# Order of the last node tiles' steps at the end of layer 2 of a two-layer graph attention kernel

## Chip, cores and metric

The kernel runs on one core of one Trainium2 chip. The metric is the device time of one execution in microseconds (us). The median of three runs of the kernel before is 2619.84 us, from 2609.17 to 2623.1.

## The reference, cut to what matters

A graph of 6250 nodes and 100000 edges, sorted by destination, passes through two graph attention layers and a small network of two dense layers; the input is added at the end.

```python
def gat_conv(x, src, dst, W, a_src, a_dst, bias, heads):
    h = (x @ W).reshape(n, heads, -1)
    alpha_s = (h * a_src[None]).sum(-1)
    alpha_d = (h * a_dst[None]).sum(-1)
    e = leaky_relu(alpha_s[src] + alpha_d[dst], 0.2)
    e = exp(e - segment_max(e, dst)[dst])
    alpha = e / (segment_sum(e, dst)[dst] + 1e-16)
    return segment_sum(h[src] * alpha[:, :, None], dst).reshape(n, -1) + bias
...
h = relu(layernorm(x))
h = relu(gat_conv(h, src, dst, W1, a_src1, a_dst1, b1, 4))   # 768 -> 256, 4 heads
h = relu(gat_conv(h, src, dst, W2, a_src2, a_dst2, b2, 1))   # 256 -> 256, 1 head
h = relu(h @ Wm1 + bm1)                                      # 256 -> 256
x = x + h @ Wm2 + bm2                                        # 256 -> 768
```

Each node has an edge to itself beside the others. All numbers are float32.

## The kernel before

The nodes lie in 49 tiles of 128 (NT = 49; the last, tile 48, holds 106 nodes). The edges lie in 784 tiles of 128, four to a group, so 196 groups (NG = 196) and four groups to a node tile. A first stage computes layer 1's features and stores them as a table of rows in device memory. Then `layer_edges` runs twice, for layer 1 and for layer 2, once over all groups each time.

In the loop of `layer_edges` over g, a group is worked on as follows.

- `gather(g + 8)` lets GpSimd (POOL) fetch the source rows of the group eight ahead, one indirect DMA for each tile of 128 edges (line 553). So the last gather is issued when g is 187, as far as the code goes.
- `pair(g, 0)` and `pair(g, 1)` take two edge tiles each: two exponentials on ScalarE (ACT; lines 620 and 622), a product, a maximum and two one-hot matrices weighted by the attention on VectorE (DVE; lines 625, 628 and 632), and two matmuls into `o_ps[g]` on TensorE (PE; line 648). In the profile, each float32 matmul stands as two records.
- `gather_up(g)` adds the group's result to a running sum (line 673) and copies a quarter of a node tile from it (line 681). When a tile's fourth quarter is there, its steps are put at the end of the list `late`. For the last group it puts the steps of the last tile, 48, there instead.
- `advance(g)` goes through `late` and lets each tile there take one piece of its steps. It is called twice in a group, and in groups 192 and 193 it goes through the list twice at each call.

What a tile does after its sum is the generator `Node2.steps`. It is cut by `yield`; the pieces are called A to F here, in program order:

- A: `all_` and its denominator `rden`, on DVE (line 896, or 906 for the last tile, and line 908).
- B: `o` on ACT (line 911), two transposes into `tp` on PE (line 761), and for the last tile the two bias rows of its outputs (line 873).
- C: `rT` on ACT (line 767), then the first dense layer on PE (line 921; "mm1" below).
- D: `mT` on ACT (line 926), then on PE, for the first half of the columns, the bias row (line 873) and two matmuls into `y_ps` (line 937).
- E: the first half's addition of the input on DVE (line 940), then bias row and matmuls of the second half on PE. A tile other than the last uses the same `y_ps` for both halves, so these wait for the addition.
- F: the second half's addition on DVE, then the tile's output DMA on SyncE's queue (SP; line 946). The last tile sends each half by itself, the first on SP at E and the second on ACT's queue at F (line 943).

After B, C, D and E stands `yield from rest(3)`: three calls of `advance` pass, the one that ran the piece among them, before the next piece is run, or one once the list `at_end` is not empty.

Nothing is reordered by a scheduler: the block runs under `tc.manual_schedule()`, and each engine gets its instructions in the order in which the Python code emits them. That order around the end of layer 2, with the calls written out, is:

```
g=193: pair(193,0) | 45 F, 46 C | pair(193,1) | 46 D | sums 191, 192
g=194: pair(194,0) | sum 193 | 46 E, 47 A | pair(194,1) | 46 F, 47 B
g=195: pair(195,0) | pair(195,1) | sum 194 | 47 C | 47 D
after: 47 E, 48 A | 47 F, 48 B | 48 C | 48 D | 48 E | 48 F
```

PSUM has two buffers for `tp` and `y_ps` of all tiles but the last (tag "n"), and three for `o_ps` and the last tile's two `y_ps` (tag "o"). The working tiles (`all_`, `o`, `rT`, `mT`, `y`) have two buffers each.

Of the kernel before, what the change touches and what calls it, by code (L numbers as in the profile page):

```python
# [30 lines left out]
NG = NQ  # L31
# [22 lines left out]
def kernel(  # L54
# [184 lines left out]
    def first_sources(layer):  # L239

        n = len(THERE[layer])
        sources[layer] = []
        for j in range(0, n, 8):
            m = min(n - j, 8)
            of = rowsp.tile([P, 16 * P], BF16, name="drow").bitcast(I32)
            nc.sync.dma_start(of[:, :m * P], bcast(src_rows, m * P, (FIRST + j) * P))
            sources[layer].append(of)
# [269 lines left out]
    def fetch_rows(r):  # L517

        if r < NET // 16:
            drow[r] = rowsp.tile([P, 16 * P], BF16, name="drow")  # L520
            nc.sync.dma_start(drow[r], bcast(dmod_d, 16 * P, r * 16 * P))
# [7 lines left out]
    def layer_edges(layer, H, node, pre, matched, pre_pool):  # L529
# [4 lines left out]
        with tc.tile_pool(name=f"eg{layer}", bufs=4) as eg, \  # L534
# [9 lines left out]
            def gather(g):  # L544
                if not 0 <= g < NG:
                    return
                for t in tiles(g):
                    k = TPG * g + t
                    if k // 2 not in G:
                        G[k // 2] = first_G[layer].get(k // 2) or rows_in(layer)  # L550
                    if k < FIRST + len(THERE[layer]):
                        continue
                    nc.gpsimd.indirect_dma_start(  # L553
                        out=G[k // 2][:, k % 2], out_offset=None, in_=table[layer],
                        in_offset=bass.IndirectOffsetOnAxis(ap=src_i[:, k:k + 1], axis=0))
# [5 lines left out]
            def make_mask(u):  # L561

                if not 0 <= u < NU:
                    return
                if layer == 2:
                    return fetch_mask(u + 1)
                a, b = (t * P for t in both(u))
                mask[u] = maskp.tile([P, 8 * P], BF16, name="mask")
                if u == 0:
                    nc.vector.memset(mask[u][:, :a], 0.0)  # L570
                at = u % 2 * 8 * P
                nc.vector.tensor_scalar(mask[u][:, a:b], drow[u // 2][:, at + a:at + b], pidx, None,  # L572
                                        ALU.is_equal)
                nc.sync.dma_start(mask_d[u * P:(u + 1) * P], mask[u])

            def make_hot(g):

                if layer == 2 or not 0 <= g < NG:
                    return
                T = tiles(g)  # L580
                k, n = TPG * g + T[0], len(T)
                hot[g] = eg.tile([P, TPG, P], F32, name="hot")
                nc.vector.tensor_tensor(  # L583
                    hot[g][:, T[0]:T[0] + n], iota_ps.unsqueeze(1).to_broadcast([P, n, P]),
                    dcol[:, k:k + n].unsqueeze(2).to_broadcast([P, n, P]), ALU.is_equal)
# [7 lines left out]
            def meet(t):  # L593

                if t >= NT:
                    return
                e_ps[t] = ps.tile([P, 16, 6 * H], F32, name="e_ps", tag="e")
                for u, at, a, b in ranges(t):
                    m = mask.pop(u)
                    for k in range(a, b):  # L600
                        nc.tensor.matmul(e_ps[t][:, at + k, :3 * H], m[:, k * P:(k + 1) * P],  # L601
                                         pre.win[:, 2 * u + k // TPG + 1], start=True, stop=True)

            def join(t):
                if t >= NT:
                    return
                (_, _, a, _), (_, at, _, b) = ranges(t)
                T = slice(a, at + b)
                nc.vector.tensor_reduce(
                    e_ps[t][:, T, 3 * H:4 * H],  # L610
                    e_ps[t][:, T, :3 * H].rearrange("p t (h k) -> p t h k", k=3), AX.X, ALU.add)
# [39 lines left out]
            def stay_warm(n):  # L651

                if layer == 1:
                    for _ in range(n):
                        nc.tensor.matmul(idle_ps[0], idle[:, :P], idle, start=True, stop=True)

            done, run, late, idle_ps = {}, {}, [], []

            def gather_up(g):

                if not 0 <= g < NG:
                    return
                last = g == NG - 1
                if last:

                    late.append(node.steps(NT - 1, None, run[0], o_ps.pop(g)))
                    return
                acc = sums.tile([P, RW[layer]], F32, name="acc")
                if g == 0:
                    nc.vector.tensor_copy(acc, o_ps.pop(g))  # L670
                else:
                    k = (g + 1) % 4
                    nc.vector.scalar_tensor_tensor(acc, run[0], keep[:, k:k + 1],  # L673
                                                   o_ps.pop(g), ALU.mult, ALU.add)
                run[0] = node.whole(NT - 1, acc) if g == NG - 2 else acc
                t, q = divmod(g - 2, 4)
                if 0 <= t < NT - 1:
                    if q == 0:
                        done[t] = sums.tile([P, RW[layer]], F32, name="sum", bufs=3)
                    r = slice(32 * q, 32 * q + 32)  # L680
                    nc.scalar.activation(done[t][r], acc[r], AF.Copy)  # L681
                    if q == 3:
                        late.append(node.steps(t, done.pop(t)))

            def advance(g):

                for _ in range(2 if NG - 4 <= g < NG - 2 else 1):
                    for step in list(late):
                        if next(step, 0) == 0:
                            late.remove(step)  # L690
# [14 lines left out]
            join(0)  # L705
            for g in range(NG):
                t, j = divmod(g, 4)
                if g == NG - 2:
                    at_end.append(g)
                gather(g + AHEAD)  # L710
                pair(g, 0)
                if g == NG - 1:
                    pair(g, 1)
                if g >= NG - 2:
                    gather_up(g - 1)
                advance(g)
                if g <= NG - 4:
                    make_hot(g + 1)
                if g in (NG - 4, NG - 3):
                    make_hot(g + 2)  # L720
                if j == 0:
                    if layer == 1:
                        fetch_rows(t + 4)
                    node.prefetch(t)
                    meet(t + 1)
                elif j == (2 if t < NT - 1 else 1):
                    node.ahead(t)
                elif j % 2:
                    make_mask((g + 7) // 2)
                if g == NG - 3:  # L730
                    idle_ps.append(ps.tile([P, 4 * P], F32, name="idle_ps", tag="e"))
                if g >= NG - 3:
                    stay_warm(3)
                if g < NG - 1:
                    pair(g, 1)
                advance(g)
                if j == 3:
                    join(t + 1)
                if g < NG - 2:
                    gather_up(g - 2)  # L740
                if g == NG - 3:
                    gather_up(g - 1)
                if NG - 3 <= g < NG - 1:
                    stay_warm(3)
                hot.pop(g, None)
                if layer == 1 and g == NG - 6:
                    first_sources(2)
            gather_up(NG - 1)
            advance(NG)
            stay_warm(4)  # L750
            if layer == 1:
# [19 lines left out]
    with tc.tile_pool(name="w2p", bufs=1) as wp, tc.tile_pool(name="wk2", bufs=2) as wk:  # L771
# [48 lines left out]
        with tc.tile_pool(name="pre1", bufs=1) as pre:  # L820
            first_hits(pre, 1, 0)
            pre1 = prepare(pre, 1, 4)
            layer_edges(1, 4, Node1(), pre1,
                        lambda: scores_in(ps, w2, *w2_in, KH, 1), pre)


    with tc.tile_pool(name="wmp", bufs=1) as wp, tc.tile_pool(name="x3", bufs=4) as xp, \
# [122 lines left out]
        for stage in range(2):  # L950
            first_hits(pre, 2, stage)
        layer_edges(2, 1, Node2(), pre2, matched, pre)

    edges_stack.close()
# [298 lines left out]
```

## Time and profile before

| what | us or value |
|---|---|
| median of three runs | 2619.84 |
| the profiled execution's own time | 2137.04 |
| its span, first to last instruction | 2135.3 |
| mean granted TensorE clock | 0.825 of full speed |
| last row gather issued on POOL | about 2111.6 |
| last matmul pair of group 195 starts | 2116.7 |
| last addition of the output starts (line 940) | 2128.68 |
| last output DMA issued (line 943) | 2129.27 |

Times in the profile count from the span's start. A line of the timeline has the start, the length, the engine, the source line, the operation, the tile it writes and those it reads, shapes and count, and in brackets how long the engine was idle before it and who released it. A line of the table by stretches has the stretch, its length, each engine's busy time and instructions, the granted clock, the share of the DMA engines and GB/s. The profiled execution is shorter than the timed runs by 483 us; the profile does not say why.

### The profile page before, as it was taken

How to read it: one execution, taken by the hardware profiler on the slowest of the kernel's cores; microseconds unless marked ns; L12 is line 12 of the kernel's file. 1: busy time of each engine (PE TensorE's matmuls, PEld its weight loads, DVE VectorE, ACT ScalarE, POOL GpSimd, SP SyncE). 2: the span in 40 equal slices, each digit the busy share in tenths (PEclk: the TensorE clock that was granted, in tenths of full speed). 3: DMA queues.
4: the chain of work that ended last, by engine and by line, in shares of the span. 5: the costliest groups of instructions: out<-in, count | busy, mean ns of one | idle time of the engine just before them, and what ended most of it. 6: DMA issues, size and time to landing. Idle time of an engine off the chain costs nothing.

```text
span 2135.3 us, 26701 instructions
## 1 busy us (share of the span) xinstructions
PE 1589.5 (74%) x6763; PEld 1075.4 (50%) x6765; DVE 1416.1 (66%) x4359; ACT 593.1 (28%) x2601; POOL 1600.6 (75%) x1759
## 2 busy tenths in 40 slices
PE   8996777766767677666768677777767777777777
PEld 6874444444444444444445445545545545545544
DVE  7887777667677777677777655555555555555554
ACT  4651222222222222222222222222222222222222
POOL 6877777777777777777777777777777777777774
PEclk9998888677777767887779888888888888888888
DMA  9976666555555565565556455565555555565553
GB/s 356 363 232 206 169 172 176 165 169 163 167 170 163 170 170 162 169 168 158 166 143 211 130 180 166 169 181 166 169 181 166 169 181 166 169 181 167 168 171 114
DMA packets 157544, 383.26 MB, mean 179 GB/s; under 512 B 35543, under 2 KB 49966, under 8 KB 157382
## 3 DMA queue, kind: packets, MB, share of 16 engines
q0 software_dynamic: 75072, 209.10, 36.6%
q1 hardware_dynamic: 80940, 170.88, 23.1%
q10 hardware_dynamic: 1370, 1.48, 0.2%
q8 instruction: 58, 0.95, 0.2%
q14 instruction: 104, 0.85, 0.1%
HBM read 323.13 MB, written 58.19 MB: 179 GB/s over the span
## 4 chain that ended last, share of the span: by engine, by line
DMA 27%; PE 26%; DVE 26%; issue 9%; ACT 7%; POOL 5%; ACTq 0%; SPq 0%; POOLq 0%; DVEq 0%
DMA G<-table,src_i 26%; PE o_ps L648 11%; DVE hw L637 8%; PE y_ps L937 7%; POOL G L553 4%; PE h_ps L350 4%; DVE acc L673 3%; DVE e_ps L625 3%; ACT sum L681 3%; DVE e_ps L635 2%; ACT e L620 2%; DVE hw L632 2%; DVE mask L572 1%; ACT e L622 1%; PE y_ps L873 1%
## 5 line engine op out<-in xcount | busy, mean ns | idle before, releaser
L553 POOL DMA_INDIRECT G<-table,src_i x1545 | 1470.1, 952 | 472.3 <-issue 260.5
L648 PE MATMUL o_ps<-hw,hot 128*128 128x260 f32 x1564 | 596.7, 520 | 282.9 <-DVE hw L637 221.4
L648 PE MATMUL o_ps<-G,hw 128*128 128x258 f32 x1564 | 469.1, 432 | 229.8 <-DVE hw L632 229.1
L648 PEld LDWEIGHTS o_ps<-hw,hot 128*128 128x128 f32 x1564 | 352.9, 248 | 492.9 <-DVE hw L637 359.2
L625 DVE TENSOR_TENSOR e_ps<-e,e_ps 128x8 f32<-128x8 f32 (+1 forms) x782 | 128.4, 164 | 598.9 <-ACT e L622 597.5
L648 PEld LDWEIGHTS o_ps<-G,hw 128*128 128x128 f32 x1564 | 309.9, 212 | 348.3 <-DVE hw L632 290.5
L681 ACT ACTIVATE sum<-acc 32x260 f32<-32x260 f32 (+1 forms) x384 | 159.9, 416 | 776.9 <-DVE acc L673 775.3
L620 ACT ACTIVATE e<-G 128x8 f32<-128x8 f32 (+1 forms) x782 | 159.9, 204 | 617.8 <-DMA G<-table,src_i 576.4
L632 DVE TENSOR_SCALAR hw<-iota_ps,dcol,w 128x128 f32<-128x128 f32 x782 | 285.0, 406 | 14.4
L637 DVE TENSOR_TENSOR hw<-G,e_ps 128x520 f32<-128x520 f32 x391 | 271.9, 695 | 15.2 <-DVE e_ps L635 2.0
L937 PE MATMUL y_ps<-wm,mT 128*128 128x384 f32 x392 | 206.5, 664 | 0.7 <-ACT mT L926 0.7
L673 DVE SCALAR_TENSOR_TENSOR acc<-acc,keep,o_ps 128x260 f32<-128x260 f32 (+1 forms) x388 | 184.5, 476 | 0.1
L622 ACT ACTIVATE e<-G 128x8 f32<-128x8 f32 (+1 forms) x782 | 148.9, 190 | 0.2
L350 PE MATMUL h_ps<-w,r 128*128 128x256 f32 x588 | 133.0, 380 | 4.4 <-ACT r L341 4.4
L583 DVE TENSOR_TENSOR hot<-iota_ps,dcol 128x512 f32<-128x512 f32 (+1 forms) x196 | 133.5, 682 | 0.0
L937 PEld LDWEIGHTS y_ps<-wm,mT 128*128 128x128 f32 x392 | 88.3, 249 | 66.9 <-issue 40.9
L350 PEld LDWEIGHTS h_ps<-w,r 128*128 128x128 f32 x588 | 108.0, 190 | 21.8 <-ACT r L341 5.7
L635 DVE TENSOR_TENSOR e_ps<-e_ps,e 128x8 f32<-128x8 f32 x391 | 68.1, 174 | 13.4
L365 POOL TENSOR_TENSOR ha<-kept,a1b 128x512 f32<-128x512 f32 x45 | 53.2, 1183 | 23.9 <-ACT kept L356 23.8
L628 DVE TENSOR_TENSOR w<-e_ps,e 128x2 f32<-128x2 f32 x391 | 62.2, 159 | 13.3
L601 PEld LDWEIGHTS <-mask 128*128 128x128 bf16 x1564 | 57.7, 101 | 11.4 <-issue 1.7
L767 ACT ACTIVATE rT<-tp,bT 128x128 f32<-128x128 f32 x196 | 59.4, 352 | 6.6 <-PE tp L761 6.4
(405 smaller groups left out, 1137.7 us busy)
## 6 DMA issues: line engine op xcount, KB each, us to landing
xt<-in_x SPq DMA_DIRECT2D x96, 384.0 KB, 4.8
drow<-dmod_d SPq DMA_DIRECT2D x49, 512.0 KB, 6.4
mask_d<-mask SPq DMA_DIRECT2D x98, 256.0 KB, 2.2
mask<-mask_d SPq DMA_DIRECT2D x98, 256.0 KB, 5.9
G<-table,src_i POOLq DMA_INDIRECT x1545, 2.9
xTt<-in_xT SPq DMA_DIRECT2D x49, 384.0 KB, 5.9
out<-y SPq DMA_DIRECT2D x48, 384.0 KB
table<-kept SPq DMA_DIRECT2D x49, 132.0 KB, 3.7
```

The costliest lines, as they stand in the source:

```text
L350: nc.tensor.matmul(h_ps, r[:, k], w1[:, k], start=(k == 0), stop=(k == KI - 1))
L553: nc.gpsimd.indirect_dma_start(out=G[k // 2][:, k % 2], out_offset=None, in_=table[layer], in_offset=bass.IndirectOffsetOnAxis(ap=src_i[:, ...
L583: nc.vector.tensor_tensor(hot[g][:, T[0]:T[0] + n], iota_ps.unsqueeze(1).to_broadcast([P, n, P]), dcol[:, k:k + n].unsqueeze(2).to_broadca ...
L620: nc.scalar.activation(e1, sc, AF.Exp)
L622: nc.scalar.activation(e2, sc, AF.Exp, scale=SLOPE)
L625: nc.vector.tensor_mul(v, e2, rho)
L632: nc.vector.tensor_scalar(hw[:, t], iota_ps, dcol[:, k:k + 1], w[:, t], ALU.is_equal, ALU.mult)
L637: nc.vector.tensor_mul(hw, Gp[:, :, :RW[1]].rearrange("p t (h c) -> p t h c", h=H), w.unsqueeze(3).to_broadcast([P, 2, H, C + 1]))
L648: nc.tensor.matmul(o_ps[g], l, r[:, :RW[layer]], start=(k == tiles(g)[0]), stop=(k == TPG - 1))
L673: nc.vector.scalar_tensor_tensor(acc, run[0], keep[:, k:k + 1], o_ps.pop(g), ALU.mult, ALU.add)
L681: nc.scalar.activation(done[t][r], acc[r], AF.Copy)
L937: nc.tensor.matmul(y_ps, mT[:, j], wm2[:, j, s * half:(s + 1) * half], start=False, stop=(j == KH - 1))
```

## The change

Only the order of the steps at the end of layer 2 is changed; layer 1 keeps its own. `at_end` is filled one group earlier, at g = 193, which ends the waiting of `rest` there. Group 194 gets a second pass of `advance` after its first, and group 195 loses its second one. After the loop the last tile's first three pieces are run before `advance` comes to the tile before it.

```diff
             for g in range(NG):
                 t, j = divmod(g, 4)
-                if g == NG - 2:
+                if g == (NG - 2 if layer == 1 else NG - 3):
                     at_end.append(g)
...
                 advance(g)
+                if layer == 2 and g == NG - 2:
+                    advance(g)
...
                     pair(g, 1)
-                advance(g)
+                if layer == 1 or g < NG - 1:
+                    advance(g)
...
             gather_up(NG - 1)
+            if layer == 2:
+
+                for _ in range(3):
+                    next(late[-1])
             advance(NG)
```

Followed through the generators by hand, this gives the order:

```
g=193: pair(193,0) | 45 F, 46 C | 46 D | pair(193,1) | 46 E | 46 F | sums 191, 192
g=194: pair(194,0) | sum 193 | 47 A | 47 B | pair(194,1) | 47 C
g=195: pair(195,0) | pair(195,1) | sum 194 | 47 D
after: 48 A, 48 B, 48 C | 47 E, 48 D | 47 F, 48 E | 48 F
```

## The prediction

> **What bounds the kernel now.** I read the page first (part 1 and the costliest groups), then a table of stretches for the end, then the timeline of the last 30 us engine by engine, then the clock in steps of 0.4 us.
>
> ```profile
> PE 1589.5 (74%) x6763; PEld 1075.4 (50%) x6765; DVE 1416.1 (66%) x4359; ACT 593.1 (28%) x2601; POOL 1600.6 (75%) x1759
> ...
> L553 POOL DMA_INDIRECT G<-table,src_i x1545 | 1470.1, 952 | 472.3 <-issue 260.5
> ```
>
> No engine is full. The row gathers set the pace: 0.95 us each and 0.30 us of issue after each, 1.25 us, so 5.0 us for the four gathers of a group and 20 us for a node tile. That pace ends with the last gather:
>
> ```profile
> 2090.00:2111.60 21.60, 16.51 (x56) 10.20 (x55) 11.54 (x41) 6.10 (x26) 16.43 (x18) 0.84 0.62 178
> 2111.60:2129.30 17.70, 15.09 (x61) 8.93 (x60) 8.53 (x25) 4.71 (x17) 0.03 (x1) 1.00 0.19 63
> 2129.30:2135.30 6.00, 0.00 (x0) 0.00 (x0) 0.00 (x0) 0.00 (x0) 0.00 (x0) 0.63 0.16 45
> ```
>
> The columns are length, busy PE, PEld, DVE, ACT, POOL, clock, DMA share, GB/s. After 2111.6 POOL is silent and PE is busy 15.09 of 17.70 us: the tail is a chain through PE with few gaps. The last 6.0 us are the output's landing and the end of the program. Only this tail, of at most 24 us (1.1% of the span), is in reach of the change. Its vector lines, of before, say what stands where:
>
> ```profile
> 2108.34 0.99 DVE L673 SCALAR_TENSOR_TENSOR acc<-acc,keep,o_ps 128x258 f32<-128x258 f32 x2
> 2110.46 0.17 DVE L625 TENSOR_TENSOR e_ps<-e,e_ps 128x2 f32<-128x2 f32 x1 [1.12 <-ACT e L622]
> ...
> 2114.34 0.56 DVE L940 TENSOR_TENSOR y<-y_ps,xt 128x384 f32<-128x384 f32 x1 [0.17 <-PE y_ps L937]
> ...
> 2120.77 0.56 DVE L940 TENSOR_TENSOR y<-y_ps,xt 128x384 f32<-128x384 f32 x1 [2.90 <-PE y_ps L937]
> 2121.25 0.41 DVE L906 TENSOR_TENSOR all__20266<-all__20245,o_ps 128x258 f32<-128x258 f32 x1
> ```
>
> The first two lines are the sums of groups 191 and 192 and the start of group 194; the third is step F of tile 46; the last two are E of tile 47 and, only behind it, A of the last tile, 48. And PE's end:
>
> ```profile
> 2115.66 2.17 PE L648 MATMUL o_ps<-G,hw 128*128 128x258 f32 x8 [0.27 <-DVE hw L632]
> 2117.67 1.05 PE L921 MATMUL tp<-rT,wm 128*128 128x128 f32 x8
> 2118.65 0.33 PE L873 MATMUL y_ps<-bm2r,ones_r 3*128 3x384 bf16 x1
> 2119.18 1.56 PE L937 MATMUL y_ps<-wm,mT 128*128 128x384 f32 x4 [0.19 <-ACT mT L926]
> 2121.38 0.32 PE L873 MATMUL y_ps<-bm2r,ones_r 3*128 3x384 bf16 x1 [0.65 <-DVE y L940]
> 2121.63 1.56 PE L937 MATMUL y_ps<-wm,mT 128*128 128x384 f32 x4
> ```
>
> Group 195 leaves PE at 2117.83 (the chain of waits goes on to mm1 there), and the last addition starts at 2128.68: 10.85 us for tiles 47 and 48, one after the other.
>
> **What the Trainium skill says.** "PSUM — Partial Sum Buffer", Engine vs sequencer instructions: the queues of ScalarE and VectorE are strictly first in, first out, and matmuls start in program order. The trace agrees: every step above stands in each engine's stream where the code emits it, so a waiting instruction holds all behind it. "TensorE: Matmul & The Clock Gate", What's actually happening: the clock is full or half, by activity in a free-running window of about 3.4 us. The trace agrees: 1.0 or 0.5, changes at about 2096.75 and 2103.6, two windows apart. Such windows were busy 1.14 of 3.41 us (33%) just before the half clock of 1854.4, and 1.88 of 3.41 (55%) at 2089.93 without one. That is where I put the threshold.
>
> **The change, part by part.** Layer 1 and everything before group 193 keep their order; no instruction is added or removed, POOL's stream is the same. Letters A to F are the steps of a tile in program order.
>
> 1. Tile 46, group 193: D goes ahead of pair (193,1), and E and F into this group's second advance, ahead of the sums of 191 and 192. Before, PE starts mm1 of tile 46 at 2107.51, and D's mT at 2108.60 lets its output matmuls start 0.42 later, at 2109.02, 1.56 long, to 2110.55. The exponentials of pair (193,1), at 2104.73 before, now queue behind mT on ACT: 2109.25; from there to the pair's first matmul it took 1.19 (2110.13 to 2111.32 for the next pair), so 2110.5, just when PE is free. Pair (193,1) issues for 0.87, to 2111.40. So far this costs about 0.2. E's addition 2110.73 to 2111.29 lies under it. Then E's bias row and matmuls: 0.3 + 1.5, to 2113.2. Now the new wait: F's addition stands at the head of VectorE's queue until 2113.2, and behind it are both sums and all of pair (194,0). From 2113.22: addition 0.56, two sums 0.99, the second sum's copy on ACT 0.46, exponential to matmul 1.19: pair (194,0) starts on PE at 2116.45. Before: 2111.32. **That is +5.13**, with PE empty from 2113.2 to 2116.45.
>
> 2. Group 194: tile 47's B ahead of pair (194,1), C ahead of group 195. Sum of 193 at 2116.63 (0.65 after the pair's hw); from that sum to B's o it took 1.68 before (2111.50 to 2113.18): 2118.31; the next exponential 0.41 later, at 2118.72; + 1.19: pair (194,1) on PE at 2119.91 (before 2114.14). The transposes, 0.38, fit before it. After it PE issues 0.87, C's mm1 0.91 and pairs (195,0) and (195,1), 0.87 each: 2123.43. Their hw are ready (2121.14 and 2122.22 by the same 1.19). Before: 2117.83. So at the end of group 195 the change stands at **+5.60**, though E and F of tile 46 (about 1.8 us of PE) and C of 47 (0.91) are already done.
>
> 3. The end. Tile 47's D has nothing to pass: nothing stands between its old and new place. Its bias row and matmuls, 0.26 + 1.56 = 1.82, go first, with mT long there. Under them A of tile 48 (0.41 + 0.17), its o (0.51) and three hops, about 1.25, are hidden; without that cover they would show in full. Then transposes to rT 0.42, rT to mm1 0.67, mm1 0.91, E's matmuls of tile 47 with the bias row 1.81 (they cover tile 48's mT, and E's addition is long done), tile 48's own 2.86, and 0.02: 8.51 against 10.85. **That is −2.34.**
>
> 4. DMAs. Tile 46's output leaves SP about 1 us earlier; nothing else is in SP's queue there. Tile 47's output moves from 2123.8 to about 2130.8, still ahead of tile 48's on SP, 2 to 3 us before the last one on ACT's queue. Before, its 0.38 MB were moved in about 1.5 us (2124.5 to 2126.0), so it should be over; I take 0, at most +1, and not below nothing, as no transfer gets shorter. Everything else after the last addition stays 6.1 us.
>
> 5. The clock, which no row of before prices here. PE is empty for 3.25 us and again from 2117.5 to 2118.9. Wherever the 3.41 us windows fall, one of them has at most 1.2 us of work, 36%: under the threshold, so the clock should halve between 2114.4 and 2118.8. From 2119.9 PE is full, and by before's records it comes back after one full window: half clock until 2123.3 to 2125.6, half of which, 1.7 to 2.9 us, is lost. I take 2.3; bounds 0 (no halving; a gain is excluded, since nothing runs above 1.0) and 11.4 (rival two).
>
> Sum: 5.60 − 2.34 + 0 + 2.3 = +5.56. The profiled execution took 2137.04 us (span 2135.3 and 1.7 around it), so 2142.6. The runs' median, 2619.84, is 483 us above the profiled execution; nothing in the trace says where these are. I carry the difference over as it is: 2619.84 + 5.56 = 2625.4. Scaled by 2619.84/2137.04 it would be +6.8.
>
> **Rivals.** *The stall is hidden, and the end's gain stays.* If in the timed runs the gathers are what is slow (483 us over 1545 gathers would be 0.31 each), pairs arrive 3.1 us apart, a group takes 6.2, and the 5 us of delay in group 194 lie largely under waits for rows; group 195 ends with its last row, as before. Then −2.3 stays: 2617.5. For it: ACT still waits for rows at 2114.30. Against: in the profile that wait is 0.42.
>
> *The half clock stays to the end*, and the kernel is measurably slower. From 2116.45 on PE has 13.4 us of work (four pairs 3.7, two mm1 1.8, transposes 0.6, output matmuls 6.2, bias rows 1.1). If no window is full, because VectorE and ACT leave gaps, all of it takes twice as long; some 2 us of gaps absorb part: +11.4, with the 3.3 of the stall +14.7: 2634.5. It decides if the gaps for rT and mT fall in every window; before, of the nine halvings after 1936 eight lasted two windows and one a single one, so I give it little.
>
> *Nothing arrives.* Gain and stall cancel, the clock holds, within 1 us: 2620.
>
> **How the numbers follow.** A difference of 0.5%, 13 us, is about what a measurement of this kernel can tell from no change. The forecast (+3 to +7) 0.62, hidden stall 0.23, nothing 0.09, half clock to the end 0.06. Only the last is a change of over 0.5%. The three runs of before spread over 14 us, so a median can stray by 6 or 7: I leave 0.03 for a stray on the good side, and 0.92 for within 0.5%, 0.05 for slower. The range goes from the hidden stall with such a stray (2611) to the half clock (2635).
>
> **What would show it.** In the profile of the changed kernel: F's addition of tile 46 right before the pair of sums, with about 1.9 us of waiting for its matmuls; PE idle some 3.2 us before pair (194,0); clock 0.5 somewhere after 2114; the last tile's A directly after the last sum, before tile 47's E; 8.5 us from the last pair's end to the last addition, or more under the half clock. I am wrong if pair (194,0) starts before 2114, if the clock holds 1.0 after a 3 us gap, or if the last transfer lands later than 6 us after the last addition.

## The result, and the profile after

The changed kernel takes 2621.14 us (median of 20 runs, 2612.03 to 2632.93), the kernel before 2616.84 (20 runs): the medians are 4.3 us apart. The ratio, taken over all runs, is 1.0020 with a 95% interval of 1.0005 to 1.0034. That is 5.2 us, between 1.3 and 8.9; 5.56 were forecast.

One thing must be known before the two profiles are laid side by side. The profiled execution of the changed kernel has a span of 2621.7 us, that of before 2135.3. This is not the change: the same programs take about 2137 us on some chips and 2610 to 2640 on others (the shorter and the longer kind below). The 20 runs of each kernel in the result are all of the longer kind, and each ratio of the experiments is of runs on one chip. Spans from different chips are not compared. What is compared is the tail, from the start of tile 46's first dense layer on PE ("mm1") to the start of the last addition. It took 21.17 us before and 27.01 after: 5.84 more. In the profile before, it begins with these lines (... stands for the lines between), mm1 of tile 46 and, 3.81 us later, the first matmuls of group 194, called pair (194,0) below:

```profile
2107.51 1.05 PE L921 MATMUL tp<-rT,wm 128*128 128x128 f32 x8
...
2111.32 1.14 PE L648 MATMUL o_ps<-G,hw 128*128 128x258 f32 x4
```

PE in the tail of the changed kernel, from the timeline:

```profile
2588.33 1.05 PE L928 MATMUL tp<-rT,wm 128*128 128x128 f32 x8
2589.31 0.33 PE L880 MATMUL y_ps<-bm2r,ones_r 3*128 3x384 bf16 x1
2589.84 1.56 PE L944 MATMUL y_ps<-wm,mT 128*128 128x384 f32 x4 [0.19 <-ACT mT L933]
2591.23 1.03 PE L648 MATMUL o_ps<-G,hw 128*128 128x258 f32 x4
2592.20 0.33 PE L880 MATMUL y_ps<-bm2r,ones_r 3*128 3x384 bf16 x1
2592.46 1.56 PE L944 MATMUL y_ps<-wm,mT 128*128 128x384 f32 x4
2597.18 1.14 PE L648 MATMUL o_ps<-G,hw 128*128 128x258 f32 x4 [3.17 <-DVE hw L632]
2599.60 0.69 PE L768 MATMUL tp<-ident,o 128*128 128x128 f32 x2 [1.28 <-ACT o L918]
2600.63 2.09 PE L648 MATMUL o_ps<-G,hw 128*128 128x258 f32 x4 [0.34 <-DVE hw L632]
```

The line numbers have moved by 7 (L921 is L928, L937 is L944, L940 is L947). The first line is mm1 of tile 46; the two halves of its output follow in the same group, with pair (193,1) between them. Then PE is empty for 3.17 us before pair (194,0), which starts 8.85 us after mm1. So of the 5.04 us by which the pair is later, about 3.2 are this gap, and 1.8 are the matmuls of tile 46's second half (0.33 and 1.56, overlapping), which stood behind the pair before and are now done ahead of it. The last line is pair (194,1), at the half clock: 2.09 us where a pair takes 1.03 to 1.14 at the full clock. VectorE says why PE was empty:

```profile
2591.43 0.56 DVE L947 TENSOR_TENSOR y<-y_ps,xt 128x384 f32<-128x384 f32 x1
2594.05 0.56 DVE L947 TENSOR_TENSOR y<-y_ps,xt 128x384 f32<-128x384 f32 x1 [2.06 <-PE y_ps L944]
2594.53 0.99 DVE L673 SCALAR_TENSOR_TENSOR acc<-acc,keep,o_ps 128x258 f32<-128x258 f32 x2
2596.32 0.17 DVE L625 TENSOR_TENSOR e_ps<-e,e_ps 128x2 f32<-128x2 f32 x1 [0.80 <-ACT e L622]
```

These are E's addition, then F's, which waits 2.06 us for E's matmuls, and behind F the two sums and the first VectorE step of pair (194,0). In the profile before, the two sums stood at 2108.34, right behind pair (193,1).

The stretches of this tail (length, busy PE, PEld, DVE, ACT, POOL, clock, DMA share, GB/s): up to F, the empty stretch, up to the end of group 195, and the end:

```profile
2588.33:2594.05 5.72, 5.50 (x23) 3.08 (x21) 1.61 (x5) 0.81 (x4) 0.00 (x0) 1.00 0.17 69
2594.05:2597.18 3.13, 0.00 (x0) 0.00 (x0) 2.22 (x7) 1.13 (x4) 0.00 (x0) 1.00 0.32 126
2597.18:2607.07 9.89, 8.26 (x27) 6.27 (x27) 5.26 (x18) 2.73 (x12) 0.00 (x0) 0.65 0.01 2
2607.07:2615.34 8.27, 7.95 (x31) 4.41 (x30) 2.26 (x5) 1.76 (x5) 0.00 (x0) 1.00 0.13 50
```

The third stretch has a mean clock of 0.65. In the last one PE is busy 7.95 of 8.27 us: the end has become a chain of PE work, as forecast.

### The profile page after: what moved, and what is told of

Read it like the earlier page. It is cut to its first block, busy times and chain, and to the rows that moved or that the text cites. A ratio compares the mean times of both kernels' runs of the same rounds, so it can differ in the third digit from the quotient of the medians.

```text
span 2621.7 us, 26701 instructions
## 1 busy us (share of the span) xinstructions
PE 1650.0 (63%) x6763; PEld 1116.7 (43%) x6765; DVE 1414.5 (54%) x4359; ACT 560.2 (21%) x2601; POOL 1604.0 (61%) x1759
## 4 chain that ended last, share of the span: by engine, by line
DVE 29%; issue 21%; PE 20%; another core or an unknown queue 19%; ACT 6%; POOL 2%; DMA 2%; ACTq 0%; POOLq 0%; SPq 0%; DVEq 0%
PE o_ps L648 9%; DVE hw L637 8%; DVE hw L632 4%; PE y_ps L944 4%; PE h_ps L350 4%; DVE acc L673 3%; DVE e_ps L625 3%; ACT sum L681 2%; POOL G L553 2%; DVE e_ps L635 2%; ACT e L620 2%; DVE mask L572 2%; DMA G<-table,src_i 2%; DVE hot L583 1%
## 5 line engine op out<-in xcount | busy, mean ns | idle before, releaser
L648 PE MATMUL o_ps<-G,hw 128*128 128x258 f32 x1564 | 497.7, 455 | 177.1 <-issue 90.4
L648 PEld LDWEIGHTS o_ps<-G,hw 128*128 128x128 f32 x1564 | 337.6, 228 | 301.4 <-issue 124.4
L944 PE MATMUL y_ps<-wm,mT 128*128 128x384 f32 x392 | 197.8, 622 | 119.3 <-issue 84.5
L944 PEld LDWEIGHTS y_ps<-wm,mT 128*128 128x128 f32 x392 | 81.7, 228 | 192.6 <-issue 138.8
L947 DVE TENSOR_TENSOR y<-y_ps,xt 128x384 f32<-128x384 f32 (+1 forms) x98 | 54.1, 552 | 127.6 <-remote 73.8
L928 PE MATMUL tp<-rT,wm 128*128 128x128 f32 x392 | 68.1, 330 | 55.8 <-ACT rT L774 44.1
L928 PEld LDWEIGHTS tp<-rT,wm 128*128 128x128 f32 x392 | 64.7, 240 | 67.2 <-ACT rT L774 50.9
L635 DVE TENSOR_TENSOR e_ps<-e_ps,e 128x8 f32<-128x8 f32 x391 | 68.2, 174 | 30.8 <-remote 12.3
```

The lines of the kernel that those rows point to most:

```text
L648: nc.tensor.matmul(o_ps[g], l, r[:, :RW[layer]], start=(k == tiles(g)[0]), stop=(k == TPG - 1))
L944: nc.tensor.matmul(y_ps, mT[:, j], wm2[:, j, s * half:(s + 1) * half], start=False, stop=(j == KH - 1))
```

## The experiments

There are ten runs, each with its own profile, and the table is read from these. The columns "pair (194,0)" and "half clock" are in us after the start of mm1 of tile 46; "half clock" is the first stretch in which the granted clock was 0.5, as far as it lies in the tail. Ratios are to before on the same chip.

| kernel | pair (194,0) | half clock | tail | ratio, 95% interval |
|---|---|---|---|---|
| before | 3.81 | none | 21.17 | 1 |
| the change | 8.85 | 11.1 to 17.9 | 27.01 | 1.0020, 1.0005 to 1.0034 |
| before again | 3.82 | none | 21.22 | one run |
| without early end | 3.82 | none | 20.15 | 0.9991, 0.9985 to 0.9997 |
| last tile only | 3.81 | none | 19.69 | 0.9987, 0.9979 to 0.9994 |
| early end only | 8.86 | 9.8 to 16.6 | 27.87 | 1.0026, 1.0016 to 1.0036 |
| late F | 6.23 | 9.3 to 12.7 | 23.12 | 1.0005, 0.9989 to 1.0022 |
| busy stall | 8.86 | none | 24.29 | 1.0023, 1.0004 to 1.0042 |
| C between pairs | 3.82 | none | 19.27 | 0.9989, 0.9973 to 1.0004 |
| the change again | 8.86 | 9.0 to 15.9 | 26.01 | 1.0017, 1.0004 to 1.0030 |
| sums between | 7.05 | 9.1 to 16.0 | 25.13 | 1.0012, 1.0003 to 1.0021 |
| C between pairs, again | 3.81 | none | 19.27 | 0.9984, 0.9977 to 0.9991 |

The theory: F's addition, put early, waits at the head of VectorE's queue and empties PE; the gap halves the clock; the last tile's early steps give 2 to 3 us back.

### Before and the change, once more

> The kernel before, unchanged, for a second profile: the first one took 2137 us where the timed runs take about 2617. The tail is measured from the start of the first dense layer's matmuls of tile 46 (mm1) to the start of the last addition: 21.17 us in the first profile of before, 27.01 in the one of the changed kernel. Theory (the order alone makes the tail): 21 to 22 us here too, even if this execution takes about 2617. Rival (the changed kernel's tail is longer because its execution was another kind of execution): about 26 to 27 us.

> The changed kernel again, unchanged, to be seen beside the others on the same chip. Theory: pair (194,0) 8.85 us after mm1 of tile 46, half clock for two windows, tail 25.5 to 28 us (27.0 in its first profile), ratio to before 1.002 to 1.003. Rival (the result rests on the other kind of execution, at 2617 us, and on one near 2137 the end's gain outweighs the stall): tail under 21 us, ratio under 1.

The second profile of before (span 2135.5) has the tail of the first within 0.05 us. The second profile of the change (span 2635.2) has its stall again to 0.01 us. Its tail is 1.0 shorter than in the first, as the half clock began 2 us earlier: pair (194,0) then fell under it and took 1.94 us instead of 1.14, but pair (194,1), which waits for other work, came no later for it (12.3 us after mm1 in both). Before itself was not profiled on a chip of the longer kind. But "C between pairs", which keeps before's order up to pair (195,0), was profiled on both kinds, and each step up to there stands in the same place within 0.01 us. So the stall depends on the order, not on the kind of chip.

### Without the early end

```diff
-                if g == (NG - 2 if layer == 1 else NG - 3):
+                if g == NG - 2:
                     at_end.append(g)
```

> The changed kernel with at_end filled at group 194 again: tile 46 keeps its places of before up to D, tile 47 and the last tile are moved as in the change. Theory (the early pieces of tile 46 make the stall, the other two moves gain): pair (194,0) starts 3.8 us after mm1 of tile 46 as before, the clock stays 1.0, the tail is 20.1 us (pair (194,1) about 1.5 later, the end 2.4 shorter), so 7 less than with the change and 1 less than before; ratio to before about 0.9996. Rival (moving tiles 47 and 48 ahead costs, tile 46 does not matter): tail 26 to 27 us, ratio 1.002.

The tail is 20.15 us, and the kernel is faster than before. Tile 46's early pieces make the loss; the other two moves bring a gain. Group 194 still pays something, in the same manner. VectorE and PE of this run:

```profile
2118.33 0.56 DVE L947 TENSOR_TENSOR y<-y_ps,xt 128x384 f32<-128x384 f32 x1 [1.20 <-PE y_ps L944]
2118.80 0.15 DVE L625 TENSOR_TENSOR e_ps<-e,e_ps 128x2 f32<-128x2 f32 x1
```

```profile
2119.65 1.14 PE L648 MATMUL o_ps<-G,hw 128*128 128x258 f32 x4 [1.15 <-DVE hw L632]
```

The extra pass of `advance` in group 194 takes tile 46's F along, ahead of pair (194,1), and PE is empty 1.15 us.

### The early end alone

```diff
-                if g == NG - 2:
+                if g == (NG - 2 if layer == 1 else NG - 3):
                     at_end.append(g)
```

(against before)

> The kernel before with only at_end filled at group 193. Theory: the whole stall and no gain: PE idle about 3.2 us before pair (194,0), which starts 8.8 us after mm1 of tile 46, the clock halves after it, tail 25 to 28 us (26.5), ratio 1.002. Rival (the stall comes from the other two moves): pair (194,0) starts 3.8 us after mm1, tail 21 us, ratio 1.000.

The full stall is there, the half clock too, and no gain: 27.87 us is the longest tail of all. PE shows it:

```profile
2111.78 1.56 PE L937 MATMUL y_ps<-wm,mT 128*128 128x384 f32 x4
2116.51 1.20 PE L648 MATMUL o_ps<-G,hw 128*128 128x258 f32 x4 [3.17 <-DVE hw L632]
2119.09 2.09 PE L648 MATMUL o_ps<-G,hw 128*128 128x258 f32 x4 [1.39 <-DVE hw L632]
```

These are the same 3.17 us as with the change. With the run before it, this settles where the loss is from.

### Which of the early pieces

```diff
-            def advance(g):
+            def advance(g, times=None):
 
-                for _ in range(2 if NG - 4 <= g < NG - 2 else 1):
+                for _ in range(times or (2 if NG - 4 <= g < NG - 2 else 1)):
...
                 if layer == 1 or g < NG - 1:
-                    advance(g)
+                    advance(g, 1 if layer == 2 and g == NG - 3 else None)
```

(against the changed kernel: D and E stay in group 193, F goes back to group 194)

> The changed kernel, except that the second advance of group 193 passes the list once: tile 46's D and E stay in group 193, F goes back to group 194. Theory (what stalls is F's addition at the head of VectorE's queue, ahead of the two sums and of pair (194,0), not the early D and E): PE waits 0.75 us instead of 3.2 before pair (194,0), which starts 6.4 us after mm1 of tile 46 (8.85 with the change, 3.8 before); the clock stays 1.0; tail 21.8 us, ratio to before 1.0003. Rival (D ahead of pair (193,1) is what delays): pair (194,0) still at 8 us or later, tail over 25.

With F away, pair (194,0) starts at 6.23, and PE is empty before it for 0.55 us only:

```profile
2615.64 1.14 PE L648 MATMUL o_ps<-G,hw 128*128 128x258 f32 x4 [0.55 <-DVE hw L632]
```

So it is F, not D or E, that empties PE. The 2.41 us by which the pair is still later than before are for the most part E's matmuls (1.82 from start to end), which PE does there instead of behind the pair. The tail missed its number, 23.12 for 21.8: the clock, which was to stay 1.0, halved for one window. The table of stretches shows the window before and the halved one:

```profile
2615.30:2618.71 3.41, 1.57 (x6) 0.88 (x6) 2.53 (x9) 1.28 (x5) 0.00 (x0) 1.00 0.29 115
2618.71:2622.12 3.41, 3.03 (x10) 2.66 (x11) 3.21 (x12) 0.82 (x6) 0.00 (x0) 0.50 0.00 0
```

A window with 1.57 us of PE work in 3.41 (46%) was followed by the half clock, though PE was empty in it for 1.28 us at most at a stretch. Yet in the change's first profile a window with less, 42%, was not; only the next one was:

```profile
2592.60:2596.01 3.41, 1.42 (x4) 0.54 (x4) 1.43 (x3) 0.85 (x3) 0.00 (x0) 1.00 0.15 61
2596.01:2599.43 3.42, 1.14 (x4) 0.68 (x4) 2.10 (x7) 1.09 (x4) 0.00 (x0) 1.00 0.14 54
```

So in these records there is no sharp bound in the share of work; the last section has the count.

The next run keeps F where the change has it, but lets the two sums go first:

```diff
                 if g == NG - 3:
                     gather_up(g - 1)
+                    if layer == 2:
+                        advance(g, 1)
```

(against the kernel just above)

> The changed kernel with the sums of groups 191 and 192 placed between tile 46's E and F instead of behind F. Theory (F's wait holds whatever is behind it; with the sums and their copies ahead of it only the pair's own work is left): pair (194,0) starts at F's addition 5.7 + 0.56 + 0.87 for the pair's three VectorE steps = 7.15 us after mm1 of tile 46 (8.85 with the change), tail 22.6 us at the full clock and up to 25 if it halves. Rival (the sums are not on the path): 8.85 and a tail of 26 to 27.

Pair (194,0) starts at 7.05; 7.15 were expected:

```profile
2117.46 1.14 PE L648 MATMUL o_ps<-G,hw 128*128 128x258 f32 x4 [1.36 <-DVE hw L632]
```

So of the 5.04 us that the change adds before pair (194,0), 1.80 are the sums and their copies behind F; the rest is F's wait for E's matmuls, its addition, and the pair's own work behind it. The tail, 25.13, includes two halved windows.

### What the clock costs

```diff
+                    stay_warm(3, 2)
                     advance(g)
...
+                if g == NG - 3:
+                    stay_warm(12, 2)
                 hot.pop(g, None)
```

(against the changed kernel, without the lines that give `stay_warm` its second argument; `stay_warm(n, 2)` issues n idle matmuls in layer 2. They are extra work and leave nothing out.)

> The changed kernel with 15 idle matmuls (bf16, 512 columns, into an unused PSUM tile, 0.216 us each at the full clock by estimate) added: 12 after tile 46's second output half, 3 after pair (194,0). They are extra work and change no value. Theory (the half clock costs 2 to 3 us of the tail): pair (194,0) stays at 8.85 us after mm1, the clock stays 1.0, tail 24.1 us against 27.0, ratio to before 1.0014. Rival (the clock costs nothing, PE waits for others anyway): tail 27 as with the change though the clock stays 1.0, ratio 1.0025.

PE's timeline here, cut at "...":

```profile
2612.15 2.75 PE L655 MATMUL idle_ps<-idle 128*128 128x512 bf16 x11
2615.48 1.14 PE L648 MATMUL o_ps<-G,hw 128*128 128x258 f32 x4 [0.58 <-DVE hw L632]
2616.46 0.81 PE L655 MATMUL idle_ps<-idle 128*128 128x512 bf16 x3
...
2618.93 1.14 PE L648 MATMUL o_ps<-G,hw 128*128 128x258 f32 x4 [0.59 <-DVE hw L632]
```

Pair (194,0) comes no sooner (8.86), but the clock stays 1.0, pair (194,1) takes 1.14 instead of 2.09, and the tail is 24.29: the halved clock cost 2.72 us in the change's first profile and 1.72 in its second. In the whole time this run cannot be told from the change: the interval of its ratio, 1.0004 to 1.0042, holds that of the change.

### The gain by itself, and a version that beats both

```diff
             gather_up(NG - 1)
+            if layer == 2:
+
+                for _ in range(3):
+                    next(late[-1])
             advance(NG)
```

(against before)

> The kernel before with only the last tile's A, B and C placed ahead of tile 47's E. Theory: everything to the end of group 195 as before, then tile 47's C and D stand before the last tile's transposes, so 1.2 us are gained at the end: tail 19.9 us, ratio about 0.9995. Rival (the last tile's matmuls ahead of tile 47's delay the end, or its early pieces add a wait): tail 21.5 us or more.

That gave 19.69 us. Then tile 47's C also goes between the pairs (195,0) and (195,1), since in the run above its mm1 and mT still follow the last pair (the lines for the last tile stay):

```diff
                 if g == NG - 1:
+                    if layer == 2:
+                        advance(g)
                     pair(g, 1)
                 if g >= NG - 2:
                     gather_up(g - 1)
-                advance(g)
+                if layer == 1 or g < NG - 1:
+                    advance(g)
```

> The kernel with only the last tile's pieces moved, and tile 47's C also placed between the pairs (195,0) and (195,1), so that its mT is ready when group 195 ends. Theory (the end is then a chain of PE work alone): pair (195,1) 0.7 us later than before, tile 47's output matmuls 0.6 earlier, tail 19.1 us (19.69 without this step), ratio to before 0.9984. Rival (the exponentials of pair (195,1) behind rT hold the pair back by more than is gained): tail 20 us or more.

> The kernel with the last tile's A, B and C ahead of tile 47's E, and tile 47's C between the pairs (195,0) and (195,1), once more, for its ratio to before. Theory (1.9 us of 2137 or 2630): 0.9985 to 0.9993, below 1 with its interval if the chip's executions scatter little. Rival (nothing is left of it in the whole time): 1.000.

The last tile's three pieces alone take 1.5 us off the tail (1.2 expected), C between the pairs another 0.4 (0.6 expected). PE's last 8 us in the first of the two runs with both:

```profile
2606.86 0.33 PE L880 MATMUL y_ps<-bm2r,ones_r 3*128 3x384 bf16 x1
2607.12 1.56 PE L944 MATMUL y_ps<-wm,mT 128*128 128x384 f32 x4
2608.52 0.38 PE L768 MATMUL tp<-ident,o 128*128 128x128 f32 x2
2608.83 0.49 PE L880 MATMUL y_ps<-bm2r,ones_r 3*128 3x384 bf16 x2
2609.61 1.16 PE L928 MATMUL tp<-rT,wm 128*128 128x128 f32 x8 [0.29 <-ACT rT L774]
2610.70 0.33 PE L880 MATMUL y_ps<-bm2r,ones_r 3*128 3x384 bf16 x1
2610.97 4.14 PE L944 MATMUL y_ps<-wm,mT 128*128 128x384 f32 x12
```

One gap of 0.29 us is left. The first run's interval touches no change (0.9973 to 1.0004); the second, on a chip of the shorter kind, has 0.9977 to 0.9991: faster than before. Its middle, 0.16%, is more than the 1.9 us of the tail explain (0.09%, the edge of the interval), so the size is better taken from the tail. By its tail it is the fastest of the versions tried.

## Why the prediction was right

The mechanism came as forecast, and each part of the sum is near its size. The table sets it against the change's first profile (and "busy stall", which parts the clock from the rest):

| part | forecast | measured | from |
|---|---|---|---|
| 1. mm1 of tile 46 to pair (194,0) | +5.13 | +5.04 | 8.85 − 3.81 |
| 2. pair (194,0) to the end of group 195, full clock | +0.47 | +0.64 | 7.15 in the busy stall − 6.51 before |
| 5. the half clock | +2.3 | +2.74 | 9.89 with the change − 7.15 |
| 3. the end | −2.34 | −2.58 | 8.27 − 10.85 |
| 4. after the last addition | 0 | −0.26 | 6.36 − 6.62 |
| sum | +5.56 | +5.58 | ratio: +1.3 to +8.9 |

That the sums agree to 0.02 us is luck: the parts miss by up to 0.44 us, both ways, the change's second profile has 1.0 us less of half clock, and the measured whole is only known to lie between 1.3 and 8.9. The end of group 195 is taken as in the prediction, at its records' end before (2117.83) and at the next matmul's start after; with the next start in both (2117.67 before), part 2 is +0.80 and part 3 −2.74, and the sum is the same. Carrying over the 483 us between profile and timed runs unchanged had no ground when it was done; the steps of equal length on both kinds of chips gave it one afterwards.

Part 1 held because it follows one queue: what stands behind F on VectorE, item by item, each with the duration that it had before. F's wait was 2.06 us, about 1.9 were forecast. The runs without F in that place (6.23) and without the sums behind it (7.05) show the same items removed singly. Part 3 held in sign and nearly in size: tile 48's A, its o and the hops were hidden under tile 47's matmuls. Part 4: tile 47's last addition, behind which its output goes, now starts 2.58 us before the last addition of all (5.45 before), and this did not hold up the end: the span goes on for 6.36 us after the last addition, 6.62 before. The −0.26 is scatter ("before again" has 6.8); and as the end lies over 6 us behind the last addition before the change too, the sign of being wrong that the prediction names there could tell nothing.

Part 5 was the least certain term and did come, in both profiles of the change. Its size depends on where the windows fall: 1.7 and 2.7 us were measured, 1.7 to 2.9 had been worked out. The threshold was the weaker half of it. It was put between 33% and 55% from two windows, but the profile before itself has a window with 1.97 us of work (58%, from 772.39) that was followed by the half clock and one with 1.49 us (44%, from 1195.65) that was not. The window that decided here had 1.14 us (33%), which is low enough by every window counted in the last section; the one before it, 42%, could have halved the clock 3.4 us sooner and did not.

The rival of the hidden stall rested on gathers that are slow one by one. On the chips of the longer kind the missing time is indeed at the gathers, but it comes in gaps, and the last gather was issued 22 us before mm1 of tile 46, so no row was late in the tail. The half clock to the end did not come either: the full clock was back after two windows. The scaling by 2619.84/2137.04, left aside in the prediction, has no ground in the tail, whose steps have the same lengths on both kinds of chips; the whole time can't tell, since its interval holds the scaled +6.8 too.

## What to carry to other kernels

When a step that waits is moved ahead in the code, list what is behind it on its in-order engine, up to the next instruction that another engine waits for; the wait and that list are the price, here 5.0 us, and the halved clock 1.7 to 2.7 more, against 2.6 gained at the end. A step whose input has only just been asked for (F right after E) is best left behind work that is ready, and the parts of such a change are worth trying singly: one of the three made the loss, the others without it beat both kernels. A gap of 3 us on PE can cost nearly as much again by the halved clock after it; idle matmuls in the gap kept the full clock here, but no gain in the whole time could be told.

## What the runs showed of the hardware that was not expected

The same program took about 2137 us on some chips and 2610 to 2640 on others. The profile's row for the row gathers, in the changed kernel's profile, of the longer kind:

```profile
L553 POOL DMA_INDIRECT G<-table,src_i x1545 | 1473.2, 954 | 885.4 <-issue 714.5
```

In the profile before, of the shorter kind, the same row had 952 ns for one gather and 472.3 us of idle time before them. One gather takes the same, but POOL's idle time before them is 413 us longer, of the 486 by which the spans differ. By the timeline, 115 gathers of the longer execution start over 2 us after the one before them, mostly 3 to 7 us and mostly after 12 to 16 at the usual 1.25; in the shorter one there is one. What makes these gaps stays open. The kernel with C between the pairs was profiled on both kinds of chips and has the gaps on one of them only, so the order of the steps does not make them.

The clock does not follow a sharp share of PE's busy time, as the records have it. In all twelve profiles it changed only at whole multiples of 3.41 us after its first change; the windows counted here lie between these points.

| window's clock | PE busy in it | windows | followed by the other clock |
|---|---|---|---|
| full | under 40% | 923 | 923 |
| full | 40 to 70% | 1610 | 474 |
| full | over 70% | 2420 | 0 |
| half | under 75% | 1334 | 0 |
| half | 75 to 95% | 810 | 322 |
| half | over 95% | 1106 | 1063 |

So under 40% of work always lost the full clock here, over 70% always kept it, and it never came back after a window with less than 75%. What decides in between stays open.
